# Seven products in place of eight in layer 1, and wider score products in layer 0, of a four-layer graph network

## The chip, the cores and the metric

The kernel runs on one core of one Trainium2 chip. The metric is the device time of one execution in microseconds; the median of several executions is compared. A core has TensorE (PE: products), VectorE (DVE), ScalarE (ACT), GpSimd (POOL) and SyncE (SP, which here only issues DMAs). They run side by side, each in its own order, and wait for each other through semaphores.

## What is computed

128 graphs of 128 nodes with 256 features go through four layers. After each, the result is added to the layer's input and normalised over the features. Cut to what matters:

```
x   : (128 graphs, 128 nodes, 256)      adj : (128, 128, 128), 0 or 1
# layer 0: attention with four score vectors, chosen by adj == 1..4
e_k = leaky_relu(einsum('bid,bjd->bij', x * a_k, x))
alpha = softmax(where(adj == k + 1, e_k, -9e15));   y = alpha @ x
# layer 1: mean of messages
h = x @ W_msg;  msg = einsum('bij,biu->bju', adj, h);  deg = adj.sum(axis=1)
y = relu(x @ W_upd + where(deg > 0, msg / max(deg, 1), 0) + bias)
# layer 2: three steps of a gated unit
m = h @ weight[i];  aggr = einsum('bst,bsd->btd', adj != 0, m)
r, z, n = gates(aggr @ w_ih.T + b_ih, h @ w_hh.T + b_hh);  h = (1 - z) * n + z * h
# layer 3: attention
Wh = x @ W;  e = leaky_relu(Wh @ a1 + (Wh @ a2).T), masked by adj > 0
y = elu(softmax(e) @ Wh)
# every layer:  x = layernorm(x + y)
```

All products are in float32, but for the aggregation of layer 2, where the features are split into three bfloat16 parts.

## The kernel before

**Tiling.** Four graphs make a group (`G = 4`), so there are 32 groups. A tile of a group has 128 partitions and 512 elements (4 x 128). Features come in two halves of 128 (`KC = 2`).

**Stages.** For each group: `loading` (L586) brings x, x in blocks for the transposition, and adj. `layer0` (L604) makes for each of the four score vectors k a mask (POOL), the scaled operand `xs` (ACT, two tiles), 8 products of 128 columns into one PSUM bank (L638), and a predicated copy into `alpha` (DVE, L639); then softmax, the product with x, the norm, and the transposed `x1T`. `layer1` (L669) multiplies each graph's `x1T` with `w_um`, which holds W_upd and W_msg side by side: two products of 512 columns per graph (L683). ACT copies the message half into `hu`, DVE adds the bias to the update half into `hu` (L684, L685). Then adj times `hu` (L689; a column of ones in `hu`, written by a memset, gives the degree), the mean, relu and norm into `xb`, and the transposed `hT`. `gru` (L719) is layer 2: three steps, each with the aggregation and the gates q, t_r, t_i, t_z. `layer3` (L893) ends with the store.

**Seven products.** The gates already use a scheme in which a product of 2 x 2 blocks takes seven block products in place of eight, with sums of the operands made beforehand: `sums` (L745) makes them as `t_h` (of h, on POOL) and `t_m` (of the aggregate, on DVE), and `gate` (L767) runs the products. Three of them go on into one running sum in PSUM, whose value in between is copied out (`snapshot`, L782) before the next product overwrites it. Such a copy has a `rush`, so that it goes early.

**Order.** Nothing is issued in the order of the program text. Every operation is recorded first (`Engine.record`, L183). `paced` (L338) gives the operations of a stage nominal times, spread between a start and an end from `TIMES`, shifted by `PERIOD` per group and by `HEAD` and `TAIL` for the first and last six groups. At the end of the kernel a planner (L1056 on) simulates the engines with estimated costs (`pe_cost` L251 and its neighbours). On each engine it issues next, of what can start, the operation with the earliest nominal time. The issue order on each engine is thereby fixed when the program is built; at run time an engine waits in that order. All operations are issued from line 232, so the profile tells them apart by their tiles' names.

**Memory.** Each tile name has a fixed number of buffers; an operation that needs a new one waits until an old one is free. PSUM has four banks called `ps` for everything but the gates, and four called `gate`. At the two ends, where fewer groups are in flight, `LENT` (L973) lets a name use another name's buffers, and `LAST` (L888) does so for the second half of the last group.

Of the kernel before, what the change touches and what calls it, by code (L numbers as in the profile page):

```python
# [18 lines left out]
def kernel(  # L19
# [231 lines left out]
    def pe_cost(op, n, out, ins, pointers, sums):  # L251
        split = any(v.buf.dtype == BF16 or v.steps[-2:-1] == (("bitcast", (BF16,), {}),) for v in ins)
        took = 0.11 if op == "transpose" else 0.056 if split else 0.005 + m_of(out[0]) / 600.0
        return took, took + 0.165
# [31 lines left out]
    def sp_cost(op, n, out, ins, pointers, sums):  # L286
# [9 lines left out]

    PERIOD = 81.73028
    EAGER, RUSH = 4.9441, 1.5064
    HOP, PE_HOP, SLACK, DMA_SLACK = 0.0975, 0.1022, 0.2622, 0.8243
    STAGES = ("loading", "layer0", "layer1", "step0", "step1", "step2", "layer3")  # L300
    TIMES = {
        "weights": ((-80.6792, -53.8982), (-234.5413, -66.3537), (-85.3398, -177.0436), (-97.3878, -222.0278), (-90.3491, -54.1657), (-171.8955, -44.6841), (-116.1849, 18.7475),),
        "loading": ((-270.5681, -253.3431), (-73.2168, -291.6634),),
        "layer0": ((-167.8607, -107.2636),),
        "layer1": ((-55.0836, 1.9826),),
        "step0": ((-0.0120, 6.9518), (0.2402, 27.6105), (15.5871, 41.1624),),
        "step1": ((50.3003, 61.9650), (57.0688, 76.7749), (63.5441, 96.9672),),
        "step2": ((105.0974, 124.9583), (122.1936, 130.3892), (118.2271, 151.0122),),
        "layer3": ((180.2686, 241.7351),),
    }  # L310
    HEAD = (
        (-8.812, -175.978, -47.271, -14.819, 0.990, 29.605, 4.780),
        (9.303, 38.059, -27.415, 8.695, 4.650, -13.814, 31.463),
        (-161.158, -14.643, 11.133, 0.523, -1.844, 22.264, 10.467),
        (-173.643, 45.499, 14.505, 11.786, 0.810, 10.190, -5.124),
        (-171.750, -3.449, 12.137, -8.917, 5.023, 2.080, 7.957),
        (-245.977, -21.192, 24.177, 5.969, 4.162, 11.377, 24.028),
    )
    TAIL = (
        (127.197, -10.789, 1.076, -13.469, 10.703, 11.032, 13.210),  # L320
        (17.815, -18.016, -1.019, -11.707, 1.115, -15.520, -14.882),
        (80.227, -2.934, 25.075, -16.097, -14.182, 5.595, 38.386),
        (92.761, -52.578, -27.642, -24.660, -19.396, -6.316, 54.637),
        (216.288, -67.705, -36.885, -29.712, 25.798, 36.675, 75.653),
        (364.741, 17.401, 10.112, 11.988, 17.448, 68.637, 12.013),
    )
# [34 lines left out]
    ident.buf.tile = ident_tile  # L361
    neg_half = tile_of("neg_half", [P, G])
    acol = tile_of("acol", [P, 4, KC])
    w_um = tile_of("w_um", [P, KC, 2 * D])
# [8 lines left out]
    w3x = tile_of("w3x", [P, KC, 2 + D])  # L373

    w_sh = tile_of("w_sh", [P, 3, 3, P])
    w_sm = tile_of("w_sm", [P, NL, 3, 3, P])

    def weights():

        POOL.memset(neg_half, -0.5)  # L380
        nats, wnat = [], []
        for src, tag, bufs in ((w_ih, "hT", 8), (w_hh, "rest", 4)):
            for g in range(0, NGC, 2):
                nat = tile_of(tag, [P, 2, D], bufs)
                ACT.dma_start(out=nat, in_=src[g * P : (g + 2) * P].rearrange("(g p) d -> p g d", p=P))
                nats.append(nat)
            if src is w_ih:
                for i in range(NL):
                    w = tile_of("hn", [P, KC, D], 3)
                    ACT.dma_start(out=w, in_=weight[i].rearrange("(c p) e -> p c e", p=P))  # L390
                    wnat.append(w)
# [36 lines left out]
        for i in range(NL):  # L428
            wT = tile_of("hT", [P, KC, D], 8)
            ps = bank()  # L430
# [38 lines left out]

        DVE.tensor_add(brz, bih[:, : 2 * KC], bhh[:, : 2 * KC])
# [60 lines left out]
    def statistics(res, tag):  # L533

        n = res.shape[1]
        mv = tile_of(f"mv_{tag}", [P, n, 2], 2)
        rstd = tile_of(f"rstd_{tag}", [P, n], 2)
        shift = tile_of(f"shift_{tag}", [P, n], 2)
        for b in range(n):
# [64 lines left out]
    def layer0(g, s):  # L604
# [11 lines left out]

        def prepared(k):
            mk = tile_of("mk", [P, G, N], 2, U8)
            POOL.tensor_scalar(mk, a_f, float(k + 1), None, op0=OP.is_equal)
            xs = []  # L620
            for c in range(KC):
                t = tile_of("xs", [P, T], 2)
                ACT.mul(t, xT[c], acol[:, k, c : c + 1])
                xs.append(t)
            return mk, xs

        ready = [prepared(0)]
        for k in range(4):
            if k < 3:
                ready.append(prepared(k + 1))  # L630
            mk, xs = ready.pop(0)
            ps = bank()
            with PE:
                PE.needs(mk)
                for b in range(G):
                    cols = slice(b * N, (b + 1) * N)
                    for c in range(KC):
                        PE.matmul(ps[:, cols], xT[c][:, cols], xs[c][:, cols], start=(c == 0), stop=(c == KC - 1))  # L638
            DVE.copy_predicated(alpha.rearrange(FLAT), mk.rearrange(FLAT), ps)  # L639

        leaky(alpha, alpha, 0.0)
        pT, rinv = softmax(alpha, "0", g == 0)
        s.x1 = res = tile_of("xa", [P, G, D], 2)
# [25 lines left out]
    def layer1(g, s):  # L669
# [7 lines left out]
        for b in range(G):  # L677
            hu.append(tile_of("hu", [P, 2 * D + 1], 2))
            POOL.memset(hu[b][:, 2 * D :], 1.0)
            ps = bank()  # L680
            with PE:
                for c in range(KC):
                    PE.matmul(ps, xT[:, b, c, :], w_um[:, c, :], start=(c == 0), stop=(c == KC - 1))  # L683
            ACT.copy(hu[b][:, D : 2 * D], ps[:, D:])  # L684
            DVE.tensor_add(hu[b][:, :D], ps[:, :D], bias_row)  # L685
        res = tile_of("xb", [P, G, D], 2)
        for b in range(G):
# [17 lines left out]
        for c in range(KC):  # L705
            t = tile_of("hT", [P, T], 8)
# [12 lines left out]
    def gru(g, s):  # L719
# [5 lines left out]
        def step(i, hT, parts):  # L725
# [18 lines left out]

            def sums(by, v, w, w_s, src, tag):  # L745


                t = tile_of(tag, [P, 4, H])
                b11, b12, b21, b22 = v[0][:, :H], v[0][:, H:], v[1][:, :H], v[1][:, H:]
# [83 lines left out]
            def update(c, z, n, d):  # L833

                DVE.scalar_tensor_tensor(d, z, 1.0, d, op0=OP.add, op1=OP.mult)
                new[c] = n if last_step else tile_of("hT", [P, T], 8)
                DVE.scalar_tensor_tensor(new[c], d, 0.5, n, op0=OP.mult, op1=OP.add)
# [22 lines left out]
            if last_step:  # L860
# [4 lines left out]
                s.way_x3 = tile_of("way_3", [G, KC, P, P], 4, F32, dram)  # L865
            of_h = sums(DVE if g + i in (0, NG + 1) else POOL, hT, w_hhT, w_sh, hT, "t_h")
            q0, q1 = gate("q", C, (of_h,), hidden, half_more)
# [20 lines left out]
    LAST = {  # L888
        "wh": ("x_in", 1), "e": ("alpha0", 1), "alpha3": ("xT", 2),
        "probT_3": ("probT_0", 1), "xd": ("x1T", 1),  # L890
    }

    def layer3(g, s, first, last):  # L893
# [49 lines left out]
        normalise(x3, shift, rstd, int(end))  # L943

        res = tile("xd", [P, n, D])
        ninv = tile_of(f"ninv_{three}", [P, n], 2)
        DVE.tensor_scalar_mul(ninv, rinv, -1.0)
        for h in range(n // 2):
# [26 lines left out]
            "x_blocks": ("t_z", 1), "x_in": ("t_i", 1), "adj_in": ("alpha3", 1), "alpha0": ("e", 1),  # L975
            "probT_0": ("probT_3", 1), "x1T": ("xd", 1), "xs": ("rT", 2),
        },
        NG - 2: {"xc": ("xa", 2), "rT": ("xT", 2)},
        NG - 1: {
            "q": ("x_in", 1), "t_r": ("x_blocks", 1), "t_i": ("xb", 2), "t_z": ("xb", 2),  # L980
            "xc": ("xa", 2), "rT": ("xs", 2),
# [7 lines left out]
    for g in range(NG):  # L989
# [3 lines left out]
        layer0(g, s)  # L993
        paced("layer0", 0, g)
        layer1(g, s)
        paced("layer1", 0, g)
        lent.clear()
        lent.update(LENT.get(g, {}) if g > 1 else {})
        gru(g, s)
        if g < NG - 1:  # L1000
            layer3(g, s, 0, G)
            paced("layer3", 0, g)
        else:

            for b in range(0, G, 2):
                layer3(g, s, b, b + 2)
                paced("layer3", 0, g)

# [21 lines left out]
    def take_slot(buf):  # L1030
        taken = slots[(buf.pool, buf.tag)]
        buf.place.remove(buf)
        if len(taken) == buf.bufs:
            taken.remove(min((b for b in taken if b.left == 0), key=lambda b: b.free_at))
        taken.append(buf)
# [98 lines left out]
```

## Time and profile before

| what | value |
|---|---|
| median of 3 runs | 2714.11 us (2712.31 to 2714.56) |
| the profiled execution's own time | 2713.67 us |
| its span, first to last instruction | 2711.9 us |
| mean granted TensorE clock | 0.997 |
| busy: PE, DVE, ACT, POOL | 98%, 81%, 67%, 59% |
| traffic with main memory | 168.44 MB read, 115.41 MB written |

The profile is of one execution. Times are in us unless marked ns. A row of a group of instructions reads: line, engine, operation, output <- inputs by tile names, shapes, xcount | busy time, mean ns of one | idle time of the engine just before them, and what ended it. PEld is the loading of weights, which runs beside PE. A float32 product appears as two MATMUL records, a bfloat16 one as one. The ends of products are modelled, so neighbouring rows overlap; the distance from start to start is the time a product takes in a stream.

### The profile page before, as it was taken

The page shows a single profiled execution, that of the slowest core. Times are in us where ns is not written, and L with a number is a line of the kernel's source. Part 1 is how long each engine was busy: PE and PEld are TensorE (multiplying, and loading weights), DVE is VectorE, ACT ScalarE, POOL GpSimd, SP SyncE. Part 2 cuts the span into 40 slices and gives each one's busy share as a digit, 9 for nine tenths or more (in the row PEclk, how much of TensorE's full clock was granted, in tenths as well). Part 3 has the DMA queues.
Part 4 walks back from the last instruction along what each step waited for, and adds up shares of the span by engine and source line. Part 5 has one row for each costly group of instructions (what it writes and reads, how often), then busy time and mean ns, then how long its engine had stood idle before and what let it go on. Part 6 is the DMA issues. An engine that isn't in the chain of part 4 may idle for free.

```text
span 2711.9 us, 45196 instructions
## 1 busy us (share of the span) xinstructions
PE 2663.1 (98%) x14340; PEld 2232.4 (82%) x14340; DVE 2187.9 (81%) x5058; ACT 1806.7 (67%) x4330; POOL 1596.5 (59%) x1538
## 2 busy tenths in 40 slices
PE   8999999999999999999999999999999999999996
PEld 6788888888887888888888888888888888888785
DVE  5777888778788887788887888887888888878877
ACT  4556776666776666766667766767767666667666
POOL 4554576654666555666556665556575555665552
PEclk9999999999999999999999999999999999999999
DMA  5535645554555455555555555555555556435441
GB/s 130 106 78 102 126 91 123 108 104 97 114 113 114 98 121 102 110 113 117 101 117 104 106 117 112 110 113 103 107 116 107 114 113 125 97 75 105 90 86 47
DMA packets 1317391, 286.89 MB, mean 106 GB/s; under 512 B 1068192, under 2 KB 1313056, under 8 KB 1317152
## 3 DMA queue, kind: packets, MB, share of 16 engines
q1 hardware_dynamic: 1314704, 281.63, 50.7%
q8 instruction: 115, 1.88, 0.3%
q10 hardware_dynamic: 2448, 2.36, 0.3%
q14 instruction: 124, 1.02, 0.1%
HBM read 168.44 MB, written 115.41 MB: 105 GB/s over the span
## 4 chain that ended last, share of the span: by engine, by line
PE 85%; DVE 9%; ACT 2%; DMA 2%; issue 1%; SPq 1%; POOL 0%; POOLq 0%; DVEq 0%; ACTq 0%
PE gate L232 58%; PE ps L232 27%; DVE z L232 1%; DVE xb L232 1%; DVE st L232 1%; DVE t_d L232 1%; SPq L232 1%; DVE rest L232 1%; DMA e<-way_f 1%; DVE t_m L232 1%; DVE t_r L232 0%; DVE xa L232 0%; DVE hT L232 0%; DMA hn<-way_h 0%; DVE t_z L232 0%
## 5 line engine op out<-in xcount | busy, mean ns | idle before, releaser
L232 POOL TENSOR_TENSOR t_r<-t_r,t_i 128x512 f32<-128x512 f32 x186 | 244.5, 1322 | 248.9 <-ACT t_i L232 164.4
L232 PE MATMUL gate<-t_h,w_hhT 128*128 128x256 f32 x1152 | 345.8, 383 | 5.1 <-ACT xb L232 2.5
L232 PE MATMUL gate<-t_m,w_sm 128*128 128x256 f32 x1152 | 342.4, 380 | 1.1 <-DVE t_m L232 0.8
L232 PE MATMUL gate<-t_m,c_gi 128*128 128x256 f32 x1152 | 341.8, 379 | 0.0
L232 PE MATMUL gate<-t_h,w_sh 128*128 128x256 f32 x1152 | 339.5, 382 | 1.8 <-ACT q L232 0.9
L232 PE MATMUL gate<-agT,c_gi 128*128 128x256 f32 x1152 | 336.1, 380 | 0.7 <-ACT t_r L232 0.6
L232 PE MATMUL gate<-hT,w_hhT 128*128 128x256 f32 x1152 | 333.7, 381 | 0.2 <-PE gate L232 0.2
L232 POOL TENSOR_TENSOR t_d<-hT,t_n 128x512 f32<-128x512 f32 x192 | 257.3, 1348 | 32.6 <-ACT t_n L232 32.1
L232 POOL TENSOR_TENSOR rstd<-rstd,neg_half 128x4 f32<-128x4 f32 x128 | 147.7, 1154 | 197.6 <-DVE rstd L232 124.7
L232 PEld LDWEIGHTS gate<-t_h,w_hhT 128*128 128x128 f32 x1152 | 208.9, 190 | 60.4 <-issue 23.2
L232 PEld LDWEIGHTS gate<-t_h,w_sh 128*128 128x128 f32 x1152 | 212.3, 190 | 54.3 <-issue 16.7
L232 PEld LDWEIGHTS ps<-xs,xT 128*128 128x128 f32 x1984 | 242.0, 193 | 12.5 <-issue 2.2
L232 PE MATMUL ps<-xs,xT 128*128 128x128 f32 x1984 | 244.2, 276 | 2.6 <-DVE xa L232 1.4
L232 PEld LDWEIGHTS gate<-t_m,w_sm 128*128 128x128 f32 x1152 | 217.1, 190 | 34.1 <-DVE t_m L232 2.2
L232 PEld LDWEIGHTS gate<-agT,c_gi 128*128 128x128 f32 x1152 | 216.8, 190 | 31.8 <-ACT t_r L232 1.2
L232 PEld LDWEIGHTS gate<-t_m,c_gi 128*128 128x128 f32 x1152 | 218.0, 190 | 30.2 <-ACT t_i L232 0.2
L232 PEld LDWEIGHTS gate<-hT,w_hhT 128*128 128x128 f32 x1152 | 214.2, 190 | 30.8 <-issue 2.9
L232 PE MATMUL ps<-w_um,x1T 128*128 128x512 f32 x496 | 232.7, 593 | 1.1 <-ACT x1T L232 1.1
L232 ACT ACTIVATE q<-gate,bhn 128x256 f32<-128x256 f32 x372 | 177.0, 476 | 81.3 <-PE gate L232 77.0
L232 POOL TENSOR_SCALAR mk<-a_f 128x512 uint8<-128x512 f32 x128 | 212.3, 1665 | 20.7 <-DVE alpha L232 13.2
L232 POOL MEMSET alpha<- 128x512 f32 (+1 forms) x63 | 33.1, 525 | 314.0 <-DVE z L232 277.8
L232 ACT ACTIVATE xs<-xT,acol 128x512 f32<-128x512 f32 x248 | 173.2, 719 | 41.2 <-PE ps L232 30.6
(231 smaller groups left out, 6668.0 us busy)
## 6 DMA issues: line engine op xcount, KB each, us to landing
way<-z SPq DMA_DIRECT2D x188, 256.0 KB, 2.4
way_h<-z SPq DMA_DIRECT2D x126, 256.0 KB, 2.4
hn<-way_h SPq DMA_DIRECT2D x504, 64.0 KB, 2.5
x_blocks<-in_x_dram SPq DMA_DIRECT2D x248, 64.0 KB, 2.5
x_in<-in_x_dram SPq DMA_DIRECT2D x31, 512.0 KB, 4.2
way_p<-z SPq DMA_DIRECT2D x62, 256.0 KB, 2.5
probT<-way_p SPq DMA_DIRECT2D x248, 64.0 KB, 2.8
hT<-way SPq DMA_DIRECT2D x248, 64.0 KB, 2.5
```

What stands on the lines that cost most here:

```text
L232: getattr(self.engine, name)(*[a.real() if isinstance(a, View) else a for a in args], **{k: a.real() if isinstance(a, View) else a for k, ...
```

## The change

- Layer 1 takes graphs in pairs. The four blocks (two graphs, two halves of features) times the four blocks of `w_um` (two halves of features, update and message) are made with seven products of 256 columns, from sums of blocks: `t` (128 x 2 x 3 x 128, in the buffer of `xd`; POOL makes it, DVE for group 0) and `w_ul` (made once, on DVE). `x1T` and `w_um` are partly overwritten by sums. Two banks serve a pair.
- `hu` is two fixed tiles; its column of ones is set once.
- Layer 0 takes two score vectors per product: `xs` holds both side by side, 16 products of 256 columns per group, in banks of two graphs, eight predicated copies of 256 elements. Masks get four buffers.
- `t_h` gets two buffers; `hT` six in place of eight; `xb` one in place of two.
- Layers 0, 1 and 3 get two plan times each; all plan constants differ; the cost of a short product has a floor in the planner.
- `LENT` and `LAST`: other names borrow, among them `t_m`, `agT` and `a_f`.

```diff
-        took = 0.11 if op == "transpose" else 0.056 if split else 0.005 + m_of(out[0]) / 600.0
+        took = 0.11 if op == "transpose" else 0.056 if split else 0.005 + max(m_of(out[0]) / 600.0, 0.2187)
...
-    PERIOD = 81.73028
+    PERIOD = 80.85697
...
-        "layer0": ((-167.8607, -107.2636),),
-        "layer1": ((-55.0836, 1.9826),),
+        "layer0": ((-168.2086, -133.2452), (-133.4706, -107.0164),),
+        "layer1": ((-54.7685, -31.0728), (-31.4045, 1.9541),),
...
-        "layer3": ((180.2686, 241.7351),),
+        "layer3": ((180.2073, 214.4257), (215.3097, 242.3797),),
...
+    hu_tiles = [work.tile([P, 2 * D + 1], F32, tag=f"hu{k}", name=f"hu{k}") for k in range(2)]
+    for hu_tile in hu_tiles:
+        nc.gpsimd.memset(hu_tile[:, 2 * D :], 1.0)
...
+        b11, b12, b21, b22 = [w_um[:, k, e : e + D] for k in range(KC) for e in (0, D)]
+        DVE.tensor_sub(w_ul[:, 0], b12, b11)
+        DVE.tensor_sub(w_ul[:, 1], b22, w_ul[:, 0])
+        DVE.tensor_sub(w_ul[:, 2], b22, b12)
+        DVE.tensor_sub(b12, b21, w_ul[:, 1])
...
-        rstd = tile_of(f"rstd_{tag}", [P, n], 2)
-        shift = tile_of(f"shift_{tag}", [P, n], 2)
+        norm = tile_of(f"norm_{tag}", [P, 2, n], 2)
+        rstd, shift = norm[:, 0], norm[:, 1]
...
-        def prepared(k):
-            mk = tile_of("mk", [P, G, N], 2, U8)
-            POOL.tensor_scalar(mk, a_f, float(k + 1), None, op0=OP.is_equal)
+        def prepared(pair):
+            masks = []
+            for k in range(2):
+                masks.append(tile_of("mk", [P, G, N], 4, U8))
+                POOL.tensor_scalar(masks[k], a_f, float(2 * pair + k + 1), None, op0=OP.is_equal)
             xs = []
             for c in range(KC):
-                t = tile_of("xs", [P, T], 2)
-                ACT.mul(t, xT[c], acol[:, k, c : c + 1])
+                t = tile_of("xs", [P, G, 2, N], 2)
+                for k in range(2):
+                    ACT.mul(
+                        t[:, :, k], xT[c].rearrange("p (b n) -> p b n", [P, G, N], b=G),
+                        acol[:, 2 * pair + k, c : c + 1],
+                    )
...
+            for h in range(2):
+                ps = bank()
+                with PE:
+                    PE.needs(*masks)
+                    for j in range(2):
+                        b = 2 * h + j
+                        for c in range(KC):
+                            PE.matmul(
+                                ps[:, j * 2 * N : (j + 1) * 2 * N], xT[c][:, b * N : (b + 1) * N],
+                                xs[c][:, b].rearrange("p k n -> p (k n)"), start=(c == 0), stop=(c == KC - 1),
+                            )
+                two = slice(2 * h, 2 * h + 2)
+                scores = ps.rearrange("p (b k n) -> p b k n", [P, 2, 2, N], b=2, k=2)
+                for k in range(2):
+                    DVE.copy_predicated(alpha[:, two], masks[k][:, two], scores[:, :, k])
 
         leaky(alpha, alpha, 0.0)
+        paced("layer0", 0, g)
...
+        t = tile_of("xd", [P, 2, 3, N])
+        by = DVE if g == 0 else POOL
+        pairs = xT.rearrange("p (h j) c n -> p h j c n", [P, 2, 2, KC, N], j=2)
+        a11, a12, a21, a22 = [pairs[:, :, j, c] for j in range(2) for c in range(KC)]
+        by.tensor_add(t[:, :, 0], a21, a22)
+        by.tensor_sub(t[:, :, 1], t[:, :, 0], a11)
+        by.tensor_sub(t[:, :, 2], a12, t[:, :, 1])
+        by.tensor_sub(a21, a11, a21)
         hu = []
-        for b in range(G):
-            hu.append(tile_of("hu", [P, 2 * D + 1], 2))
-            POOL.memset(hu[b][:, 2 * D :], 1.0)
-            ps = bank()
-            with PE:
-                for c in range(KC):
-                    PE.matmul(ps, xT[:, b, c, :], w_um[:, c, :], start=(c == 0), stop=(c == KC - 1))
-            ACT.copy(hu[b][:, D : 2 * D], ps[:, D:])
-            DVE.tensor_add(hu[b][:, :D], ps[:, :D], bias_row)
-        res = tile_of("xb", [P, G, D], 2)
+        for h in range(2):
+            one, two = [tile_of("hu", [P, 2 * D + 1], 2) for _ in range(2)]
+            hu += [one, two]
+            shared, other = bank(), bank()
+            sums = shared[:, :D]
...
+            product(sums, xT[:, 2 * h, 0, :], w_um[:, 0, :D], first=True)
+            snapshot(DVE.tensor_add, one[:, :D], sums, bias_row)
+            product(shared[:, D:], xT[:, 2 * h, 1, :], w_um[:, 1, :D], last=True)
+            product(sums, t[:, h, 1], w_ul[:, 1])
+            snapshot(ACT.copy, one[:, D : 2 * D], sums)
+            DVE.tensor_add(one[:, :D], one[:, :D], shared[:, D:])
+            product(other[:, :D], t[:, h, 0], w_ul[:, 0], first=True)
+            product(sums, xT[:, 2 * h + 1, 0, :], w_ul[:, 2])
+            snapshot(ACT.copy, two[:, D : 2 * D], sums)
+            DVE.tensor_add(two[:, D : 2 * D], two[:, D : 2 * D], other[:, :D])
+            product(sums, xT[:, 2 * h + 1, 1, :], w_um[:, 0, D:], last=True)
+            DVE.tensor_add(two[:, :D], sums, bias_row)
+            product(other[:, :D], t[:, h, 2], w_um[:, 1, D:], last=True)
+            DVE.tensor_add(one[:, D : 2 * D], one[:, D : 2 * D], other[:, :D])
+        paced("layer1", 0, g)
+        res = tile_of("xb", [P, G, D], 1)
...
-            of_h = sums(DVE if g + i in (0, NG + 1) else POOL, hT, w_hhT, w_sh, hT, "t_h")
+            of_h = sums(DVE if g + i in (0, NG + 1) else POOL, hT, w_hhT, w_sh, hT, "t_h", 2)
...
-        "wh": ("x_in", 1), "e": ("alpha0", 1), "alpha3": ("xT", 2),
+        "wh": ("x_in", 1), "e": ("alpha0", 1), "alpha3": ("x_blocks", 1),
...
-            "probT_0": ("probT_3", 1), "x1T": ("xd", 1), "xs": ("rT", 2),
+            "probT_0": ("probT_3", 1), "x1T": ("xc", 1), "a_f": ("rT", 2),
...
-            "q": ("x_in", 1), "t_r": ("x_blocks", 1), "t_i": ("xb", 2), "t_z": ("xb", 2),
+            "q": ("x_in", 1), "t_r": ("x_blocks", 1), "t_m": ("x1T", 1), "agT": ("a_f", 2), "t_i": ("xb", 1),
```

Inside `layer1`, `product` is one PE product into the given columns and `snapshot` runs its operation with the planner's `rush`, as in the gates.

More of the change, by code (lines that the diff above doesn't have):

```diff
@@ L294 @@
     engines = (PE, DVE, ACT, POOL, SP)
-    PERIOD = 81.73028
-    EAGER, RUSH = 4.9441, 1.5064
-    HOP, PE_HOP, SLACK, DMA_SLACK = 0.0975, 0.1022, 0.2622, 0.8243
+    PERIOD = 80.85697
+    EAGER, RUSH = 5.0382, 1.5184
+    HOP, PE_HOP, SLACK, DMA_SLACK = 0.1011, 0.0400, 0.1473, 0.9844
     STAGES = ("loading", "layer0", "layer1", "step0", "step1", "step2", "layer3")
     TIMES = {
-        "weights": ((-80.6792, -53.8982), (-234.5413, -66.3537), (-85.3398, -177.0436), (-97.3878, -222.0278), (-90.3491, -54.1657), (-171.8955, -44.6841), (-116.1849, 18.7475),),
-        "loading": ((-270.5681, -253.3431), (-73.2168, -291.6634),),
-        "layer0": ((-167.8607, -107.2636),),
-        "layer1": ((-55.0836, 1.9826),),
-        "step0": ((-0.0120, 6.9518), (0.2402, 27.6105), (15.5871, 41.1624),),
-        "step1": ((50.3003, 61.9650), (57.0688, 76.7749), (63.5441, 96.9672),),
-        "step2": ((105.0974, 124.9583), (122.1936, 130.3892), (118.2271, 151.0122),),
-        "layer3": ((180.2686, 241.7351),),
+        "loading": ((-271.7676, -204.9849), (-136.5164, -357.7858),),
+        "layer0": ((-168.2086, -133.2452), (-133.4706, -107.0164),),
+        "layer1": ((-54.7685, -31.0728), (-31.4045, 1.9541),),
+        "step0": ((-2.4931, 2.4355), (-0.2977, 18.0086), (16.1471, 40.9206),),
+        "step1": ((46.2681, 58.9066), (54.6560, 84.9368), (63.9135, 96.7103),),
+        "step2": ((103.2730, 125.4613), (122.4888, 131.5979), (117.2911, 150.5442),),
+        "layer3": ((180.2073, 214.4257), (215.3097, 242.3797),),
+        "weights": ((-51.6037, -39.3564), (-292.7491, -166.2959), (70.1689, -176.7787), (-41.7902, -379.5116), (81.7725, -31.0245), (-162.0511, -4.2110), (-268.0433, 2.9372),),
@@ L310 @@
     }
     HEAD = (
[L312 to L317, printed above, removed]
+        (-142.107, -344.069, -33.032, -27.571, -10.832, 34.843, 9.524),
@@ L318 @@
+        (-14.570, -18.935, -31.216, -11.691, 21.264, 0.827, 45.868),
+        (-82.917, -49.547, 29.893, 10.323, 10.619, 12.025, 18.221),
+        (-48.038, 41.867, 11.148, 10.972, 1.431, 12.124, -2.817),
+        (18.421, -8.537, 14.927, 2.354, -2.271, 4.917, 4.988),
+        (41.987, -21.335, -6.499, -22.644, 2.521, 13.648, 2.218),
     )
     TAIL = (
-        (127.197, -10.789, 1.076, -13.469, 10.703, 11.032, 13.210),
-        (17.815, -18.016, -1.019, -11.707, 1.115, -15.520, -14.882),
-        (80.227, -2.934, 25.075, -16.097, -14.182, 5.595, 38.386),
@@ L323 @@
-        (92.761, -52.578, -27.642, -24.660, -19.396, -6.316, 54.637),
-        (216.288, -67.705, -36.885, -29.712, 25.798, 36.675, 75.653),
-        (364.741, 17.401, 10.112, 11.988, 17.448, 68.637, 12.013),
+        (278.925, -30.108, -19.729, -22.018, -11.283, 14.111, 7.552),
+        (140.713, -8.189, -0.100, 11.811, 8.954, -7.964, -23.428),
+        (170.710, 2.974, -7.319, -10.206, -6.662, -4.236, -3.433),
+        (337.019, -64.103, -24.048, -10.827, -26.270, -11.392, 51.351),
+        (571.071, -90.799, -52.642, -5.790, 62.743, 49.485, 209.272),
@@ L326 @@
+        (357.729, 28.154, 1.444, 49.673, 45.151, 110.194, 169.665),
     )
@@ L373 @@
     w3x = tile_of("w3x", [P, KC, 2 + D])
+    w_ul = tile_of("w_ul", [P, 3, D])
     w_sh = tile_of("w_sh", [P, 3, 3, P])
@@ L381, in weights @@
         nats, wnat = [], []
-        for src, tag, bufs in ((w_ih, "hT", 8), (w_hh, "rest", 4)):
+        for src, tag, bufs in ((w_ih, "hT", 6), (w_hh, "rest", 4)):
             for g in range(0, NGC, 2):
@@ L428, in weights @@
         for i in range(NL):
-            wT = tile_of("hT", [P, KC, D], 8)
+            wT = tile_of("hT", [P, KC, D], 6)
             ps = bank()
@@ L624, in prepared @@
                 xs.append(t)
-            return mk, xs
+            return masks, xs
         ready = [prepared(0)]
[L628 to L631, printed above, removed]
-            ps = bank()
-            with PE:
-                PE.needs(mk)
-                for b in range(G):
-                    cols = slice(b * N, (b + 1) * N)
-                    for c in range(KC):
-                        PE.matmul(ps[:, cols], xT[c][:, cols], xs[c][:, cols], start=(c == 0), stop=(c == KC - 1))
-            DVE.copy_predicated(alpha.rearrange(FLAT), mk.rearrange(FLAT), ps)
+        for pair in range(2):
+            if pair == 0:
+                ready.append(prepared(1))
+            masks, xs = ready[pair]
+            for h in range(2):
[13 more added lines that the diff above has]
+                    DVE.copy_predicated(alpha[:, two], masks[k][:, two], scores[:, :, k])
@@ L675, in layer1 @@
         DVE.tensor_scalar(s.a_ne, a_f, 0.0, None, op0=OP.not_equal)
-        hu = []
-        for b in range(G):
-            hu.append(tile_of("hu", [P, 2 * D + 1], 2))
-            POOL.memset(hu[b][:, 2 * D :], 1.0)
-            ps = bank()
-            with PE:
-                for c in range(KC):
-                    PE.matmul(ps, xT[:, b, c, :], w_um[:, c, :], start=(c == 0), stop=(c == KC - 1))
-            ACT.copy(hu[b][:, D : 2 * D], ps[:, D:])
-            DVE.tensor_add(hu[b][:, :D], ps[:, :D], bias_row)
@@ L686, in layer1, with product, snapshot @@
-        res = tile_of("xb", [P, G, D], 2)
+        t = tile_of("xd", [P, 2, 3, N])
[6 more added lines that the diff above has]
+        by.tensor_sub(a21, a11, a21)
+        hu = []
+        for h in range(2):
[3 more added lines that the diff above has]
+            sums = shared[:, :D]
+            def product(cols, data, weights, first=False, last=False):
+                PE.matmul(cols, data, weights, start=first, stop=last, skip_group_check=True)
+            def snapshot(engine, *args):
+                engine(*args)
+                ops[-1].rush = 1.0
+            product(sums, xT[:, 2 * h, 0, :], w_um[:, 0, :D], first=True)
[12 more added lines that the diff above has]
+            DVE.tensor_add(one[:, D : 2 * D], one[:, D : 2 * D], other[:, :D])
@@ L705, in layer1 @@
         for c in range(KC):
-            t = tile_of("hT", [P, T], 8)
+            t = tile_of("hT", [P, T], 6)
             cols = slice(c * P, (c + 1) * P)
@@ L743, in step, with sums @@
             H = T // 2
-            def sums(by, v, w, w_s, src, tag):
-                t = tile_of(tag, [P, 4, H])
+            def sums(by, v, w, w_s, src, tag, bufs=1):
+                t = tile_of(tag, [P, 4, H], bufs)
                 b11, b12, b21, b22 = v[0][:, :H], v[0][:, H:], v[1][:, :H], v[1][:, H:]
@@ L835, in update @@
                 DVE.scalar_tensor_tensor(d, z, 1.0, d, op0=OP.add, op1=OP.mult)
-                new[c] = n if last_step else tile_of("hT", [P, T], 8)
+                new[c] = n if last_step else tile_of("hT", [P, T], 6)
                 DVE.scalar_tensor_tensor(new[c], d, 0.5, n, op0=OP.mult, op1=OP.add)
@@ L943, in layer3 @@
         normalise(x3, shift, rstd, int(end))
+        paced("layer3", 0, g)
         res = tile("xd", [P, n, D])
@@ L993 @@
         layer0(g, s)
-        paced("layer0", 0, g)
+        paced("layer0", 1, g)
         layer1(g, s)
-        paced("layer1", 0, g)
+        paced("layer1", 1, g)
         lent.clear()
@@ L1001 @@
             layer3(g, s, 0, G)
-            paced("layer3", 0, g)
+            paced("layer3", 1, g)
         else:
@@ L1006 @@
                 layer3(g, s, b, b + 2)
-                paced("layer3", 0, g)
+                paced("layer3", 1, g)
     order = {}
@@ L1032, in take_slot @@
         buf.place.remove(buf)
+        gone = None
         if len(taken) == buf.bufs:
-            taken.remove(min((b for b in taken if b.left == 0), key=lambda b: b.free_at))
+            gone = min((b for b in taken if b.left == 0), key=lambda b: b.free_at)
+            taken.remove(gone)
+        if buf.tag == "hu":
+            buf.tile = gone.tile if gone else hu_tiles[len(taken)]
         taken.append(buf)
```

## The prediction

> **What bounds the kernel now.** I read the page's engine shares and slices first, then one period in the middle by engine, then the order of time on PE, where the step from one row's start to the next is what a product really costs, and last the two ends. One group of four graphs takes 81.7 us in the middle: the first aggregation of successive groups starts at 1453.7, 1535.4, 1617.1, 1698.8, 1780.5 and 1862.2 us in the timeline.
>
> ```profile
> span 2711.9 us, 45196 instructions
> PE 2663.1 (98%) x14340; PEld 2232.4 (82%) x14340; DVE 2187.9 (81%) x5058; ACT 1806.7 (67%) x4330; POOL 1596.5 (59%) x1538
> PE   8999999999999999999999999999999999999996
> PEclk9999999999999999999999999999999999999999
> ```
>
> PE is full from the second slice to the last but one, at an undisturbed clock. The same by stages (columns: stretch, length, busy time and count of PE, weight loads, DVE, ACT, POOL, then clock and DMA):
>
> ```profile
> 1081.70:1163.40 81.70, 81.70 (x445) 69.20 (x444) 67.41 (x157) 56.47 (x137) 50.17 (x48) 1.00 0.54 111
> 0.00:100.00 100.00, 86.67 (x453) 66.40 (x454) 61.71 (x154) 48.97 (x110) 48.42 (x55) 0.98 0.55 118
> 2600.00:2711.90 111.90, 90.16 (x456) 74.35 (x454) 85.55 (x187) 69.65 (x174) 40.18 (x36) 0.95 0.23 52
> ```
>
> In the middle PE has no idle time at all; DVE has 14.3 us of it per period, ACT 25.2, POOL 31.5. So there, time moves only with PE's own work, until some other engine's extra work makes PE wait. At the ends PE idles 13.3 us in the first 100 and 21.7 us in the last 112: those are chains of single steps. A busy PE may hide small bubbles, so I price by starts:
>
> ```profile
> 1043.35 1.95 PE L232 MATMUL ps<-xs,xT 128*128 128x128 f32 x16
> 1045.14 0.60 PE L232 MATMUL gate<-t_h,w_hhT 128*128 128x256 f32 x2
> ...
> 1046.00 0.22 PE L232 MATMUL ps<-a_ne,xb 128*128 128x128 bf16 x1
> ...
> 1046.67 0.65 PE L232 MATMUL gate<-hT,w_sh 128*128 128x256 f32 x2
> ```
>
> Two records are one product in f32. Eight score products of 128 columns take 1045.14 - 1043.35 = 1.79 us, 0.224 each. Twelve bf16 products of 128 columns take 1046.67 - 1046.00 = 0.67 us, 56 ns each.
>
> ```profile
> 1230.78 1.88 PE L232 MATMUL ps<-w_um,x1T 128*128 128x512 f32 x4
> 1232.49 0.59 PE L232 MATMUL gate<-t_h,w_sh 128*128 128x256 f32 x2
> 1232.93 0.59 PE L232 MATMUL gate<-t_m,w_sm 128*128 128x256 f32 x2
> 1233.36 1.03 PE L232 MATMUL ps<-hu,a_f 128*128 128x257 f32 x4
> ```
>
> One graph of layer 1 (two products of 512 columns) takes 1.71 us; a product of 256 columns takes 0.432 (1232.93 - 1232.49, and 1233.36 - 1232.93).
>
> **The change, part by part.** *Layer 1's products.* Before: four graphs at 1.71 = 6.85 us of PE. After: two pairs of graphs with seven products of 256 columns each, 14 x 0.432 = 6.05. Saved: 0.80 us per group. Here the Trainium skill speaks against the change ("TensorE: Matmul & The Clock Gate", section "Back-to-back issue gap"): in a stream of weight loads and products it gives 81 ns at 128 columns and 131 ns at 512, so narrow products cost more per column. The row first: 56 ns for 128 columns in bf16, and in f32, per record, 112 ns at 128 (1.79/16) and 428 at 512 (1.71/4), that is 2 x 56 and 2 x 214, almost strictly with the columns. By the page (98 ns at 256 as my estimate between its two figures, two such per record) layer 1 would go from 16 x 2 x 131 = 4.2 us to 28 x 2 x 98 = 5.5, a loss of 1.3. By the rows it gains 0.80. The trace is of this very stream, so I take the rows.
>
> *Layer 0's scores.* Before: 32 products of 128 columns, 4 x 1.79 = 7.16 us. After: 16 of 256, 16 x 0.432 = 6.91. Saved: 0.25. Together 1.05 us of 81.7 per group; times 31 (group 0 runs in the chain-bound head, where PE time counts for little) = 32.6 us.
>
> *What DVE gets.* The rows, mean ns after the comma:
>
> ```profile
> L232 DVE COPY_PREDICATED alpha<-mk,ps 128x512 f32<-128x512 uint8 x124 | 90.3, 728 | 70.9 <-PE ps L232 67.9 <-POOL t_d L232 1.5 <-POOL a_f L232 1.4
> L232 DVE TENSOR_TENSOR hu<-ps,bias_row 128x256 f32<-128x256 f32 x128 | 52.5, 410 | 58.7 <-PE ps L232 56.1 <-ACT hu L232 2.1
> L232 POOL TENSOR_TENSOR t_h<-hT,t_h 128x256 f32<-128x256 f32 x188 | 175.6, 934 | 7.3
> L232 POOL TENSOR_TENSOR t_h<-hT 128x256 f32<-128x256 f32 x188 | 146.7, 796 | 41.5 <-PE gate L232 35.7 <-DVE hT L232 4.1 <-DMA hT<-way 1.4
> ```
>
> Layer 1's four additions of 128x256 become ten: +6 x 0.410 = 2.46 us. Four predicated copies of 512 become eight of 256; no row has that size, bounds are 0.364 (half the row, +0) and 0.49 (the 410 ns row plus the 0.08 by which 728 lies above the 651 of a plain 512-element copy from PSUM), so 0 to +1.0; I take +0.45 by the nearest, the 410 row. DVE: 67.4 + 2.9 = 70.3 of a period of about 80.7, 87% where it was 83%. Still 10 us idle, so on PE's path this is nothing by itself; it makes DVE's queue longer ahead of the steps PE does wait for (t_m, the split of hn, alpha).
>
> *What POOL gets.* Four sums of 128x256 (796 and 934 ns rows: 3.2 to 3.7 us) against four memsets of hu less (about 0.1 each): 50.2 + 3.1 = 53.3 of 80.7, 66%. They wait for x1T's landing; behind them on POOL stand masks, t_h sums, t_d and t_r of the groups in their steps, and PE waits for t_h. POOL idles 31 us per period, so 0. ACT: layer 1's four copies stay four; the score operands stay eight of 128x512 (719 ns), with a strided output; 0 to +0.1 each, I take 0. No DMA is added or removed; those of loading only move within SP's queue.
>
> *New waits.* Each half of layer 1 now has three copies out of a sum that the next product overwrites: PE must wait for each. Behind that product stand the gate products of other groups. What an uncovered one costs is visible where the work runs out, at the end:
>
> ```profile
> 2608.87 0.59 PE L232 MATMUL gate<-t_m,w_sm 128*128 128x256 f32 x2
> 2609.92 0.70 PE L232 MATMUL gate<-t_h,w_hhT 128*128 128x256 f32 x2 [0.46 <-ACT xb L232]
> ```
>
> The step is 1.05 instead of 0.43: 0.62 us. The gates have three such copies each, 36 per period, and yet PE is at 81.70 of 81.70, so the order in which the planner mixes groups covers them; layer 1 brings six more. I allow 0.12 us per period, 3.7 in all (bounds: 0, and 6 x 0.62 = 3.7 per period). The first score product of a pair now waits for two masks and four operands instead of one and two; layer 0 has tens of us of lead, so 0.
>
> *Buffers.* The second t_h removes POOL's wait for PE (35.7 us idle before t_h): POOL is not the bound, 0; next in line there is the landing of hT. hT from eight to six: a step's old pair is last read by gate z and t_d, just before the new pair is written, so two groups in steps and one in layer 1 need about six; 0, at worst a late update. xb from two to one: it is held from its first write at 1234.88 to the last aggregation's end at 1292.05, 57 us, and next written at 1316.58; 24 us of slack, 0. xd is now shared by layer 1's sums and layer 3's result (held 1259.35 to its store at 1285.73, again from 1341.80): 52 us free, where layer 1's products, spread over some 60 us now, must be bunched; the plan gives its first part 23.7 us. 0, if that holds. The two plan times only reorder; rstd and shift in one tile are the same instructions: 0.
>
> *The ends.* Head: four more weight sums on DVE (1.6 us) and group 0's four sums on DVE (1.7), then a longer chain product, copy, product; against it, less PE work. I take +1.5 (bounds -3 and +5). Tail: more borrowed buffers (t_m, agT, one xb) for the last group. Of its 21.7 us of idle PE most is a chain through softmax, layer 3 and the norm that borrowing does not shorten; I take -1.5 (bounds -6 and +3).
>
> **The sum.** 2713.7 (span 2711.9 and 1.8 around it; the median of the runs is 0.4 higher) - 32.6 + 3.7 + 1.5 - 1.5 = 2684.8; against the median 2685.
>
> **Rivals.** *A, the forecast*: 2685, chance 0.74; by its bounds 2672 to 2697. *B, half is lost*: DVE at 87% delays releases, and of layer 1's six copies one per group stands uncovered (0.62 x 31 = 19 us in place of 3.7): 2700, chance 0.15. For it: DVE already sets alpha, t_m and xb; against: 10 us idle. *C, slower*: the banks. Layer 1 now holds two of the four ps banks through seven products and their copies, where it held one for two products; scores, aggregations and layer 3 share the other two, PE runs in order, and the copies come uncovered. It decides from 1.05/0.62 = 1.7 uncovered copies per group; at three, +0.8 x 31 = +25: 2739, chance 0.07. Against it: the gates do the same with banks of their own, at no visible cost. *D, nothing*: the reordering loses at the ends and in irregular DMA waits what PE gains, 2714, chance 0.04. It needs 30 us, more than the whole idle time of the tail; unlikely.
>
> Faster by over 0.2% (5.4 us, about what a measurement here can tell from no change): A, B and little else, 0.89; within it 0.03; slower 0.08. The range takes A's bounds and B: 2670 to 2704.
>
> **What would show it.** Right: the period about 80.8 us, score products in steps of 0.43, layer 1 with 28 records per group at 0.216, PE still without idle time in the middle, DVE near 87%. Wrong: steps of about 1.05 at layer 1's products with an ACT or DVE release on hu (B, C); PE waiting on a ps bank with layer 1's banks held (C); a period of 81.7 (D); the ends longer than 13 and 22 us of idle PE.

## The result, and the profile after

The changed kernel takes 2682.28 us (median, 2679.59 to 2684.14) against 2713.21 (2712.04 to 2714.56): a ratio of 0.9885, with a 95% interval of 0.9868 to 0.9902. The profiled execution took 2682.21 us with a span of 2680.4. It moved as forecast, by 31 us where 28.9 was worked out. The terms of that sum came out differently, though.

The page's engine shares and the windows by stage, as shown of before (one period in the middle, the first 100 us, the last 112):

```profile
PE 2630.7 (98%) x13700; PEld 2266.0 (85%) x13700; DVE 2222.2 (83%) x5386; ACT 1790.8 (67%) x4330; POOL 1658.9 (62%) x1536
```
```profile
1105.40:1186.00 80.60, 80.60 (x426) 70.36 (x425) 67.89 (x167) 55.34 (x137) 52.41 (x49) 1.00 0.54 113
0.00:100.00 100.00, 80.41 (x359) 61.13 (x360) 72.49 (x192) 49.95 (x109) 54.13 (x57) 0.98 0.59 126
2568.50:2680.40 111.90, 90.70 (x455) 74.44 (x453) 79.46 (x186) 72.33 (x182) 37.44 (x35) 0.93 0.25 57
```

The period is 80.6 us, 1.1 less, and PE is still without idle time there. In the head PE now idles 19.6 us (13.3 before), in the last 112 us 21.2 (21.7). From 1000 to 1900 us the profile shows no wait of PE above its mark, so the sign of rival C, PE waiting for a bank, is absent. The products by their starts, scores and then layer 1:

```profile
1191.78 1.89 PE L232 MATMUL ps<-xs,xT 128*128 128x256 f32 x8
1193.50 0.59 PE L232 MATMUL gate<-hT,w_hhT 128*128 128x256 f32 x2
```
```profile
1237.41 0.59 PE L232 MATMUL ps<-w_ul,xd 128*128 128x256 f32 x2
1237.84 1.03 PE L232 MATMUL gate<-hT,w_hhT 128*128 128x256 f32 x4
1238.70 0.59 PE L232 MATMUL gate<-t_h,w_hhT 128*128 128x256 f32 x2
1239.14 0.59 PE L232 MATMUL ps<-w_ul,x1T 128*128 128x256 f32 x2
```

Four score products take 1.72 us. Between two products that share a running sum (1237.41 and 1239.14) stand three gate products, 1.30 us; they cover the copy on ACT, which ran from 1238.04 to 1238.41.

For an account of the whole span I give every PE record the median step of its shape (112 ns for 128 columns, 216 for 256, 217 and 218 for 257 and 258, 429 for 512, 56 for bf16), sum them as PE's work, and call what the starts are further apart the excess. Worked out from the two traces, in us:

| | before | after | difference |
|---|---|---|---|
| PE's work | 2622.9 | 2588.6 | -34.3 |
| excess, first 200 us | 21.4 | 27.4 | +6.0 |
| excess, 200 to 1000 | 17.4 | 10.9 | -6.5 |
| excess, 1000 to 1900 | 7.9 | 5.7 | -2.2 |
| excess, 1900 to the last 112 | 10.2 | 15.3 | +5.1 |
| excess, last 112 us | 16.4 | 16.3 | -0.1 |
| before the first and after the last product | 15.7 | 16.2 | +0.5 |

### The profile page after: what moved, and what is told of

Read it like the earlier page. It is cut to its first block, busy times and chain, and to the rows that moved or that the text cites. A ratio compares the mean times of both kernels' runs of the same rounds, so it can differ in the third digit from the quotient of the medians.

```text
span 2680.4 us, 44283 instructions
## 1 busy us (share of the span) xinstructions
PE 2630.7 (98%) x13700; PEld 2266.0 (85%) x13700; DVE 2222.2 (83%) x5386; ACT 1790.8 (67%) x4330; POOL 1658.9 (62%) x1536
## 4 chain that ended last, share of the span: by engine, by line
PE 90%; DVE 5%; ACT 2%; issue 1%; SPq 0%; DMA 0%; POOL 0%; POOLq 0%; DVEq 0%; ACTq 0%
PE gate L232 61%; PE ps L232 28%; DVE z L232 0%; SPq L232 0%; DVE t_m L232 0%; DVE t_d L232 0%; ACT t_z L232 0%; DVE st L232 0%; DVE rest L232 0%; DVE alpha L232 0%; DVE xb L232 0%; ACT agT L232 0%; DVE t_z L232 0%; DVE t_r L232 0%; ACT xs L232 0%
## 5 line engine op out<-in xcount | busy, mean ns | idle before, releaser
L232 POOL TENSOR_TENSOR t_h<-hT 128x256 f32<-128x256 f32 x188 | 147.5, 802 | 321.6 <-DVE hT L232 254.0
L232 PE MATMUL gate<-t_m,c_gi 128*128 128x256 f32 x1116 | 330.9, 379 | 0.0
L232 PE MATMUL gate<-t_m,w_sm 128*128 128x256 f32 x1116 | 327.9, 379 | 0.1
L232 PE MATMUL gate<-agT,c_gi 128*128 128x256 f32 x1116 | 325.6, 379 | 0.0
L232 PEld LDWEIGHTS gate<-t_h,w_hhT 128*128 128x128 f32 x1152 | 215.9, 190 | 37.6 <-ACT t_z L232 4.5
L232 PE MATMUL ps<-xs,xT 128*128 128x256 f32 x1024 | 241.5, 380 | 4.4 <-ACT xs L232 3.9
L232 POOL TENSOR_TENSOR norm<-norm,neg_half 128x4 f32<-128x4 f32 x128 | 155.0, 1211 | 142.9 <-DVE norm L232 112.8
L232 PEld LDWEIGHTS ps<-xs,xT 128*128 128x128 f32 x1024 | 193.4, 190 | 33.0 <-ACT xs L232 5.7
L232 ACT COPY t_r<-gate 128x256 f32<-128x256 f32 x279 | 102.7, 368 | 174.4 <-PE gate L232 174.1
L232 POOL TENSOR_SCALAR mk<-a_f 128x512 uint8<-128x512 f32 x124 | 192.6, 1562 | 3.3
```

The costliest lines, as they stand in the source:

```text
L232: getattr(self.engine, name)(*[a.real() if isinstance(a, View) else a for a in args], **{k: a.real() if isinstance(a, View) else a for k, ...
```

## Experiments

My theory: time is PE's work plus what an order fixed in advance leaves uncovered. The rivals: the seven products' copies eat part of the gain (B, C); or the gain is one of order and buffers, not of products. Differences below are to 2682.3; the kernel before took 2712.8, 2713.1 and 2714.2 in the three groups of runs, so some 1 us is drift. Edits are to the changed kernel. "Kept order" means that the same calls stand in the same order on each engine; the others were ordered anew by the planner.

### Each part alone

**Layer 1 with eight products, ordered anew.**

```diff
-        t = tile_of("xd", [P, 2, 3, N])
...
-            product(other[:, :D], t[:, h, 2], w_um[:, 1, D:], last=True)
...
+            for c in range(KC):
+                PE.matmul(ps, xT[:, b, c, :], w_um[:, c, :], start=(c == 0), stop=(c == KC - 1))
```

> The changed kernel with layer 1 as before: eight products' worth (two of 512 columns per graph), no sums of x1T and no w_ul; all else, plan times and buffers too, as changed; the planner orders anew. If PE's own work sets the time (my theory): 0.80 us more PE work per group, a period of 81.4 us instead of 80.6 and +25 us, 2707. If layer 1's copies out of running sums or the four sums on POOL cost time that the changed kernel pays somewhere (rivals B and C), this kernel is free of them and comes out less slow: +10 to +18, about 2695. The head should show it: group 0 no longer waits on hu's chain, so 2 to 3 us come back there.

Measured: 2753.3, ratio to before 1.0146 (1.013 to 1.0163), +71. Both expectations missed. PE's work rose by 26.2 us as reckoned; the excess rose in every stage, from 5.7 to 24.7 between 1000 and 1900. This kernel says more of its order than of its products.

**The same PE work in the kept order.** `again()` issues the call just recorded a second time, unknown to the planner.

```diff
             product(sums, xT[:, 2 * h, 0, :], w_um[:, 0, :D], first=True)
+            again()
```

> The changed kernel in its own order, with the first product of each pair in layer 1 run twice (it overwrites, so nothing else changes): 16 products of 256 columns per group, which is the PE work of layer 1 before (6.91 us against 6.85). The layer-1-as-before kernel lost 71 us and was ordered anew; this one keeps the order. If what that kernel lost beyond 25 us was its new order: here +0.86 x 32 = +27 us, 2709, period 81.5. If layer 1's seven products are hidden in bubbles that the copies leave anyway: 0 to +10.

Measured: 2713.6, ratio 1.0004 (0.9995 to 1.0013), +31.3; PE's work +27.7 of it. One product more per pair takes all of the gain back. With 1.5 us more of PE's work this kernel is 40 us faster than the one above, though that one has less to do on DVE and POOL: what it lost beyond PE's work came mostly with its order. (The two also differ in how layer 1 uses its banks; no run parts that from the order.)

**Score products of 128 columns, kept order.**

```diff
-                        for c in range(KC):
-                            PE.matmul(
-                                ps[:, j * 2 * N : (j + 1) * 2 * N], xT[c][:, b * N : (b + 1) * N],
-                                xs[c][:, b].rearrange("p k n -> p (k n)"), start=(c == 0), stop=(c == KC - 1),
-                            )
+                        for k in range(2):
+                            for c in range(KC):
+                                PE.matmul(
+                                    ps[:, (2 * j + k) * N : (2 * j + k + 1) * N], xT[c][:, b * N : (b + 1) * N],
+                                    xs[c][:, b, k], start=(c == 0), stop=(c == KC - 1),
+                                )
```

> The changed kernel with the score products of 128 columns again, into the same places of the same banks, with the planner told the same cost, so that the order on every engine is the changed kernel's. Only the width of the products differs. By the rows of before: 32 x 0.224 - 16 x 0.432 = +0.25 us per group, +8 us, 2690. By the Trainium skill's figures for a stream of weight loads and products (81 ns at 128 columns): 64 x 2 x 81 ns = 10.4 us per group against 6.9 measured, +3.5 per group, +100 us. If weight loads at 128 columns cost nothing and PE has other slack: 0.

Measured: 2688.9, ratio 0.9912 (0.9897 to 0.9927), +6.6. The period is 80.8. So layer 0's wider products are worth 0.2 us per group. Below, 16 records of 128 columns take 1.79 us, 112 ns each, against 216 for 256 columns: the weight loads of 128 columns hide almost wholly. The 81 ns per product that the Trainium skill gives for such a stream ("TensorE: Matmul & The Clock Gate", section "Back-to-back issue gap"), counted twice per record as in the prediction, would make 162; it does not apply to this stream:

```profile
1194.20 1.95 PE L232 MATMUL ps<-xs,xT 128*128 128x128 f32 x16
1195.99 0.60 PE L232 MATMUL gate<-hT,w_hhT 128*128 128x256 f32 x2
```

### How much cover there is

**Layer 1's copies twice, kept order** (`again()` in `snapshot`).

> The changed kernel in its own order, with each of layer 1's six copies out of a running sum done twice in a row (about 0.4 us longer each until the next product may start). Covered copies, as my prediction took them (0.12 us per group allowed): 0 to +4 us. Just covered, without reserve: +0.2 to +1.0 us per group, +7 to +32. Uncovered (rivals B and C): 6 x 0.4 = 2.4 us per group, +77.

Measured: 2720.4, ratio 1.0031 (1.0019 to 1.0044), +38. The period is 82.0: of 6 x 0.4 = 2.4 us more, PE lost 1.4. The same place as above:

```profile
1254.31 0.59 PE L232 MATMUL ps<-w_ul,xd 128*128 128x256 f32 x2
1254.74 1.03 PE L232 MATMUL gate<-hT,w_hhT 128*128 128x256 f32 x4
1255.61 0.59 PE L232 MATMUL gate<-t_h,w_hhT 128*128 128x256 f32 x2
1256.23 0.70 PE L232 MATMUL ps<-w_ul,x1T 128*128 128x256 f32 x2
```
```profile
1254.94 0.78 ACT L232 COPY hu<-ps 128x256 f32<-128x256 f32 x2 [0.85 <-PE ps L232]
1255.76 0.42 DVE L232 TENSOR_TENSOR hu<-hu,ps 128x256 f32<-128x256 f32 x1
```

The three gate products now end at 1256.04 (by the step of 0.43), and the next product of the sum starts 0.19 later. Even here the doubled copy on ACT is over at 1255.72; what ended last is DVE's addition from the same bank, at 1256.18, some 0.4 us later after the product at 1254.31 than in the changed kernel. Taken over nine periods, the steps before the products that go on in a sum lost only 0.6 us per period. As much was lost one stage on, at adj times `hu`, which waits for DVE's last addition into `hu`:

```profile
1260.72 0.70 PE L232 MATMUL ps<-hu,a_f 128*128 128x257 f32 x2 [0.34 <-DVE hu L232]
```

So at the sums three quarters of the added time stay covered, and the later use of `hu` is as tight as they are. In all, 0.4 us more per copy costs more than rival B had put the loss at.

**Predicated copies twice, kept order** (`again()` after `copy_predicated`).

> The changed kernel in its own order, with every predicated copy of layer 0 done twice: +3.5 us of DVE work per group (8 x 0.434), more than the change itself brought, about 88% busy, and unknown to the order. If DVE's slack is real and the 135 us of the kernel with eight more additions came from its new order: 0 to +10 us. If DVE is what binds near 90%: +1 us or more per group, +32 or more.

Measured: 2726.3, ratio 1.0052 (1.0039 to 1.0065), +44: excess +11.9 in the first 200 us, +12.0 to 1000, +7.0 to 1900, +13.0 up to the last 112. DVE from 1000 to 1900 (first row the changed kernel):

```profile
1000.00:1900.00 900.00, 900.00 (x4745) 785.55 (x4744) 758.62 (x1860) 620.12 (x1510) 588.26 (x538) 1.00 0.53 111
```
```profile
1000.00:1900.00 900.00, 899.25 (x4713) 776.35 (x4712) 784.03 (x1928) 615.50 (x1494) 575.66 (x529) 1.00 0.53 110
```

Over the whole run each added us on DVE (3.5 per group, 112 in all) cost 0.4. In the middle it cost less than half of that: the period is 81.2, 0.6 us for 3.5, at a DVE that is 87% busy; most of the 44 us was lost outside the steady middle. So "still 10 us idle" is a reserve for most of the added work there, but not for what stands ahead of a step PE waits for.

**Eight more additions on DVE, ordered anew** (`DVE.tensor_add(x1[:, b], x1[:, b], x1[:, b])`, two per graph, after x1's last use).

> The changed kernel with eight more additions of 128x256 on DVE per group in layer 1, onto x1 after its last use, known to the planner: +3.3 us of DVE per period, 90 to 91% busy, more than the change itself brought. If DVE has slack (my theory, which put the change's 2.9 us at nothing): 0 to +4 us in all. If DVE's queue is already near what delays PE (rival B): +0.5 us or more per group, +15 us or more.

Measured: 2817.4, ratio 1.0381 (1.0365 to 1.0396), +135, three times the run above for no more work. Periods alternate between 82.0 and 84.1. Here the new order, and x1's buffer being held longer, are added to DVE's load; this run cannot part them.

**The sums on POOL twice, kept order** (`again()` after three of the four `by.tensor_...`; group 0's are on DVE).

> The changed kernel in its own order, with three of the four sums of x1T on POOL done twice: +2.3 us of POOL work per group, known to no plan. POOL is at 65% in the middle; my prediction put the sums at nothing: 0 to +4 us in all. If POOL's queue too is only just in time, as DVE's and ACT's turned out to be (about 0.4 us lost per us added on DVE, 0.6 on the copies): +0.9 us per group, +29.

Measured: 2693.7, ratio 0.9928 (0.9916 to 0.9941), +11.4. From 1000 to 1900 the excess is 6.2 instead of 5.7: POOL has its slack there. The cost is +3.8 in the first 200 us, +4.5 to 1000 and +3.4 after 1900; the first of these holds group 0's, so it is not POOL's alone.

### Order and buffers

**One buffer for t_h, ordered anew** (`"t_h", 1`).

> The changed kernel with one buffer for t_h (4 KB left unused), ordered anew. My prediction put the second t_h at nothing, since POOL is not the bound: 0 to +3 us, 2682 to 2685. The rival: the middle of the changed kernel has fewer bubbles than before because h's sums are made ahead of the gates; then without the second buffer the bubbles of before come back, +8 us or more.

Measured: 2908.3, ratio 1.0722 (1.0705 to 1.0738), +226; the largest effect of all. Who PE waited for from 1000 to 1900, total, times and longest:

```profile
PE gate L232 <- POOL t_h L232: 38.7, 18, 3.8
PE gate L232 <- ACT q L232: 11.0, 18, 0.7
```

In the changed kernel PE has no such wait above the profile's mark in that stretch. The longest of these waits ends at 1071.06. POOL before it:

```profile
1065.45 1.50 POOL L232 TENSOR_SCALAR mk<-a_f 128x512 uint8<-128x512 f32 x1
1066.92 1.04 POOL L232 TENSOR_TENSOR rest<-rest 128x512 bf16<-128x512 f32 x1
1067.93 1.92 POOL L232 TENSOR_SCALAR mk<-a_f 128x512 uint8<-128x512 f32 x1
1069.82 2.31 POOL L232 TENSOR_TENSOR t_h<-hT 128x256 f32<-128x256 f32 x2
```

PE's last product with the old sums had started at 1064.52, and the profile shows no idle time of POOL that PE ended from 1000 to 1900 (before it does, 11 times, 8.2 us in all). So here PE does not wait for the buffer itself but for the place of h's sums in POOL's order, behind two masks and a split. The kernel before lived with one buffer. Why this plan puts the sums so late, and what one buffer costs in an order made for it, no run shows.

**One plan time per stage, ordered anew.**

```diff
-        "layer1": ((-54.7685, -31.0728), (-31.4045, 1.9541),),
+        "layer1": ((-54.7685, 1.9541),),
```
(and so for layers 0 and 3)

> The changed kernel with one plan time each for layers 0, 1 and 3 (from the start of the first part to the end of the second), ordered anew. My prediction: two plan times only reorder, 0, if layer 1's sums in xd stay clear of layer 3's result in the same buffer. If the sharing of xd needs the second time, layer 3 and layer 1 now wait for each other: +0.5 us or more per group, +16 or more. Since three kernels ordered anew were 46 to 226 us above their PE work, a loss of +30 to +150 would fit a plan that suits one set of costs only.

Measured: 2706.8, ratio 0.9976 (0.9967 to 0.9986), +24.5. In the middle nothing changed: a period of 80.6, an excess of 5.9. Nearly all of it lies at the end: +13.5 from 1900 to the last 112, +9.8 in those. The sharing of xd does not need the second time.

**The last group's borrowing as before, ordered anew** (no `t_m`, no `agT`; `t_z` in `xb`).

> The changed kernel without the last group's new borrowing: t_m and agT use their own buffers, t_z borrows xb as before, ordered anew. My prediction gave the ends' borrowing and order together -1.5 us. If the borrowing is what keeps the last 112 us at before's idle time: +5 to +15 here, all of it after 2500 us. If it does nothing: 0 to +2. The middle should stay at a period of 80.6.

Measured: 2688.9, ratio 0.9908 (0.9893 to 0.9923), +6.6, with +7.2 of excess in the last 112 us and at most 1.1 of change in any other stretch.

**No priority for layer 1's copies, ordered anew** (`rush` left out).

> The changed kernel without the priority of layer 1's copies out of running sums, ordered anew. With the copies twice as long 1.4 us per group came uncovered, so they are just covered as they stand. If the priority is what covers them: +0.3 us or more per group, +10 or more. If the nominal times alone cover them: 0 to +5, but for what a new order brings at the ends.

Measured: 2698.6, ratio 0.9945 (0.9933 to 0.9958), +16. The middle is untouched (5.7): PE runs the changed kernel's order for its first 13000 records of 13700, so the nominal times cover the copies by themselves; +15.1 lie in the last 112 us, where a new order fell worse.

**Group 0's operands on two engines, kept order but for the two that move.**

```diff
+                    if g == 0 and pair == 0 and k == 1:
+                        DVE.tensor_scalar_mul(t[:, :, k], src, by)
+                    else:
+                        ACT.mul(t[:, :, k], src, by)
```

> The changed kernel in its own order, with group 0's first two operands of k = 1 scaled on DVE instead of ACT, so that the first score product waits for two scalings on ACT and not for four. PE waits 2.76 us there, the longest new wait of the head. If the head's waits add to the end: -1.0 to -1.5 us. If PE catches up with them later, out of work that waits anyway: 0. The interval will be about 3 us wide, so the trace must tell: the wait before the first score product 1.3 us shorter, and whether the first aggregation of group 9 comes earlier.

Measured: 2684.1, ratio 0.9891 (0.9878 to 0.9905). It missed: the first score product waits longer, not shorter. The changed kernel, then this one:

```profile
19.85 3.90 PE L232 MATMUL ps<-xs,xT 128*128 128x256 f32 x16 [2.76 <-ACT xs L232]
```
```profile
23.15 5.72 PE L232 MATMUL ps<-xs,xT 128*128 128x256 f32 x16 [4.76 <-DVE xs L232]
```

On DVE the scaling stands behind weight sums and a copy of adj:

```profile
21.69 0.56 DVE L232 TENSOR_TENSOR w_sh<-w_hhT,w_sh 128x384 f32<-128x384 f32 x1
22.17 1.23 DVE L232 TENSOR_SCALAR xs<-xT,acol 128x512 f32<-128x512 f32 x2
```

Still it tells something: the first aggregation of group 0 came 2.8 us later, that of group 9 2.1, and the span ended 2.1 later (one execution each). In this order, what is lost in the head is not caught up. None of the twelve beats the changed kernel.

## Why the prediction was right, point by point

**PE's work: right.** -34.3 us against -32.6. Some 1 us of the difference is group 0, which I had left out; the account counts its work, but with PE idle for 19.6 us there, whether its time was saved is not shown. Layer 0: 6.6 us measured, 8 reckoned. Layer 1: one product per pair too many costs 31.3 us, 27.7 of it PE's work; 0.80 x 31 = 24.8 were reckoned for the slightly smaller difference to before (6.85 us of PE against the 6.91 of this run). The two, less 1.9 us for that, make 36 of a gain of 31: by this estimate, which takes them to add up, the rest of the change cost some 5 us.

**The row against the rule: right.** The Trainium skill's figures for a stream (the section named above) would have made layer 1 a loss and layer 0 a gain of 3.5 us per group; 0.2 was measured there.

**New bubbles, 3.7: none in the steady middle.** The excess per period stayed at 0.5 us (81.7 - 81.2 before, 80.6 - 80.1 after, with PE's work per group from the same steps). What fell, 8.7 us from 200 to 1900, lies in periods that were not steady: the changed kernel keeps its period from group 9 on, the one before only from group 13 on, and with one period of 82.7 after that. What delays the kernel before there is open; no run took it apart.

**The ends, +1.5 and -1.5: mis-sized.** The head measured +6.0, the last 112 us -0.1, and the groups before those, for which the sum had no term, +5.1. The head's waits of PE, as far as they are new:

```profile
PE ps L232 <- ACT xs L232: 3.9, 3, 2.8
PE ps L232 <- DVE xb L232: 3.9, 1, 3.9
PE ps L232 <- DVE hu L232: 2.3, 3, 1.6
```

Before, these rows were 0.7, 1.0 and none. "The first score product of a pair now waits for ... four operands ... layer 0 has tens of us of lead, so 0" holds in the middle and fails for group 0, which has no lead. The wait for hu is the chain I had named; that on xb follows group 0's norm, which stood some 0.8 us behind a mask on POOL. The +5.1 after 1900 sits where the last six groups have shifted plan times; how much of it belongs to which shift is open. I had most of the tail as a chain that borrowing does not shorten; the runs showed that the new borrowing is worth 7 us in the last 112, and two plan times 23 after 1900, in the orders that came with them.

**Edits costed at nothing.** DVE's load: 84% (67.9 of 80.6 us), not 87. The new rows came as reckoned (415 to 433 ns each), but others became shorter, t_d from 894 to 799 ns and rT from 956 to 666 (1000 to 1900 us), and one longer, the sum of xb and xa from 791 to 1206; why is open. DVE's slack: nearly right in the middle (0.2 us lost per us added), wrong over the whole run (0.4). POOL's: right in the middle, wrong outside it. The second t_h: wrong in this plan; it was judged by POOL's idle time, while what matters is when POOL, in its order, comes to the sums that PE waits for. "The two plan times only reorder": right in the middle, wrong at the end. The shared xd, the one xb and the six hT were not tried alone; the steady middle, with the excess per period unchanged, shows no cost of them.

**Two sums that do not come out.** Eight predicated copies at 410 ns against four at 728 are 0.37 us more, not 0.45. The upper bound of 2697 does not follow from the bounds named: with the bubbles at 3.7 and the ends at +5 and +3 it is 2693. The result hangs on neither.

The forecast was right because its main term was. That it came within 3 us is luck: a gain of 8.7 us of excess in the middle and a loss of 11 us in the head and after 1900, neither foreseen at that size, nearly cancelled.

## What to carry to other kernels

Where one engine is full in the middle and the order is fixed in advance, price a change by that engine's steps from start to start; that term holds to a few us. Treat the idle time of the others not as a reserve but as cover with a place: ask, for each added us, which step of the full engine stands behind it. And when such a kernel is tested by undoing a part, keep the order, or the test measures the planner.

## What the runs showed of the hardware that was not expected

A long wait of PE can cost more than itself. With one t_h buffer, the wait of 3.8 us is followed by products in slow steps, at half the granted clock (the column before the DMA share, 1.00 and then 0.50):

```profile
1071.06 1.22 PE L232 MATMUL gate<-t_h,w_hhT 128*128 128x256 f32 x2 [3.79 <-POOL t_h L232]
1072.87 1.22 PE L232 MATMUL gate<-t_h,w_sh 128*128 128x256 f32 x2 [0.59 <-POOL t_h L232]
```
```profile
1000.00:1066.00 66.00, 64.80 (x330) 55.23 (x330) 55.48 (x131) 42.23 (x106) 40.44 (x36) 1.00 0.51 107
1071.00:1077.00 6.00, 4.13 (x7) 2.00 (x8) 3.00 (x8) 0.95 (x2) 5.76 (x7) 0.50 0.57 119
```

The pair lasts 1.22 us where 0.59 was usual, and the granted clock from 1000 to 1900 us is 0.95 instead of 1.00. A clock 5% lower over 900 us is some 45 us (an estimate), of an excess of 117.6 there; the named waits make up 55.0. Shorter waits did not do it: in the run with eight more additions the longest wait of PE in that stretch is 1.3 us, and the clock stays at 1.00.
